# Layer 0 of a four-layer chain: two images' score products interleaved with half of the value sums of two parts back, and stores sent together

## The chip, the cores and the metric

One core of one Trainium2 chip runs the whole chain as one program. The metric is the device time of one execution in microseconds (us). Engines are named as in the profile: PE is TensorE's matmul and PEld its weight load, DVE is VectorE, ACT is ScalarE, POOL is GpSimd, SP is SyncE, which here only issues DMAs.

## The reference

The input is four images of 16 channels, 512 by 512, in float32. Four layers follow each other. Layer 0 is window attention with an MLP; layers 1 to 3 are convolutions (a quantised one with batch statistics, a residual pair of 3x3 convolutions, and a 3x3 convolution with an MLP on 128 hidden channels). Only layer 0 is touched by the change:

```python
def _L0_conv_ref(x, ...):
    x = x + depthwise_3x3(x) + pos_b                 # per channel
    xt = tokens(x); shortcut = xt
    win = windows_of_8x8(aff(xt, alpha1, beta1, color1))   # 64 tokens a window
    q, k, v = heads(win @ qkv_w.T + qkv_b)           # 2 heads of 8 channels
    attn = softmax(einsum('bhnd,bhmd->bhnm', q * 8 ** -0.5, k), axis=-1)
    out = einsum('bhnm,bhmd->bhnd', attn, v) @ proj_w.T + proj_b
    x = shortcut + back(out)
    h1 = gelu(aff(x, alpha2, beta2, color2) @ fc1_w.T + fc1_b)
    return x + (h1 @ fc2_w.T + fc2_b)
...
x = layer0(x); x = layer1(x); x = layer2(x); x = layer3(x)
```

There are 4 x 64 x 64 windows of 64 tokens in layer 0.

## The kernel before, in words

**Steps and parts.** Layer 0 (`window_attention`) works in 64 steps. One step holds 64 columns of 8 rows in each of 8 strips of the four images. The partitions are four groups of 32, called quads: quad u is image u, and it holds two strips of 16 channels. The strips of one image make four pairs `vv`. A step is cut into eight parts k = 0 to 7: part k is strip pair k // 2 and four of its eight windows, for all four images and both strips.

**One part.** `scores(k)` makes 16 score products, one for each image u and window jj. Each reads 32 rows (quad u) and all 128 columns of the array, and writes 128 columns of `bank(u)`; images 0 and 1 share the PSUM tile `pairs[0]`, images 2 and 3 share `pairs[1]`. ACT then takes the exponential of each pair into the tile `e`. `values(k)` turns the values with four 128x128 transposes into a bank, and ACT or DVE copies them into one of three tiles `yts`, beside columns of ones. `attend(e, k)` makes the 32 sums of values and of weights: each reads 64 rows (one strip, w = 0 or 1) and 32 columns (one image) and writes to one of two banks, 4 and 5 for even k, 6 and 7 for odd k. `divide` transposes both banks on DVE (the tile `a`), takes the reciprocal of the sums on DVE, and multiplies on POOL; `turn_back` transposes the quotient on DVE into `o`.

Since the operands are float32, the trace shows each of these products as two passes: a weight load and a matmul, twice. A product of 32 rows and 128 columns is shown as the shape 32*128, one of 64 rows and 32 columns as 64*32.

**The order.** The engines' queues follow the order in which the Python code emits (`manual_schedule`). In the step's loop over k = 1 to 7 the order is:

```python
es[k] = scores(k, n)
values(k)
attend(es[k - 1], k - 1)
ts[k - 1] = divide(k - 1, n, nc.gpsimd)
if 1 < k < 7:
    turn_back(ts[k - 2], k - 2)
if k % 2 and more:
    turn_keys(ys[n + 1], k // 2)
highest_output()
send(5)
```

`turn_keys` issues eight DMAs from SP that write the keys of the next step into `y2` once part k has been read. `send(5)` issues up to five stores of the finished output tile `xo`, from SP. `highest_output` takes one maximum of the output on DVE into `peak`, over 512 values a partition (eight of them for every two steps). Before the loop the step runs `values(0)`, `scores(0)` and `output` (the second matmul of the MLP of the step before, line 432, whose sums DVE writes to `xo`, line 437). After the loop come `attend` of part 7, the remaining divisions, and a stretch of products of 32 rows and 32 columns: depthwise taps (`depthwise`, line 287) and queries (`query`, line 319) for later steps, the projection (`project`, line 409) and the first matmul of the MLP (`hidden`, line 421). ACT changes its table of functions twice in a step, before and after the exponentials.

**Lines of the profile.** Line 353 is the score product, 361 the exponential, 338 the transpose of the values, 344 and 346 their copy on ACT and on DVE, 374 the sums, 389, 394 and 396 the three parts of `divide`, 403 `turn_back`, 452 `highest_output`, 90 a store, 310 a DMA of `turn_keys`. Lines 1047 to 1217 are the matmuls of layers 1 to 3.

Of the kernel before, what the change touches and what calls it, by code (L numbers as in the profile page):

```python
# [12 lines left out]
F32 = mybir.dt.float32  # L13
BF16 = mybir.dt.bfloat16
AF = mybir.ActivationFunctionType
# [9 lines left out]
B, C, H, W = 4, 16, 512, 512  # L25
P = 128
# [5 lines left out]
WS = 8  # L32
# [111 lines left out]
def window_attention(ctx: ExitStack, tc, xw, x1, hots, m, v, peak):  # L144
# [14 lines left out]
    nc = tc.nc  # L159
    U = V = 4  # L160
    BW = 64
# [10 lines left out]
    pairs = [ps.tile([P, 2, 512], F32, name=f"pair{i}") for i in range(2)]  # L172
    singles = [ps.tile([P, 512], F32, name=f"bank{i}") for i in range(4)]

    def bank(i):
        return pairs[i // 2][:, i % 2, :] if i < 4 else singles[i - 4]

    def quad(i):
        return slice(32 * i, 32 * i + 32)
# [81 lines left out]
    px = ctx.enter_context(tc.tile_pool(name="w0x", bufs=2))  # L261
# [6 lines left out]
    y2 = pa.tile([P, V, NJ, 2, T], F32, name="y2")  # L268
    nc.gpsimd.memset(y2, 0.0)
    g = pa.tile([P, V, NJ, NH, T], F32, name="g")  # L270
    o = pa.tile([P, V, NJ, NH, T], F32, name="o")
    most = pa.tile([P, STEPS], F32, name="most")
    yts = [pa.tile([P, 4 * U, 3, C], F32, name=f"yt{i}") for i in range(3)]
# [59 lines left out]
    def values(k):  # L333

        vv, jl = k // 2, 4 * (k % 2)
        b, t = bank(4 + 2 * (k % 2)), yts[k % 3]
        for jj in range(4):
            nc.tensor.transpose(  # L338
                b[:, P * jj : P * jj + P],
                y2[:, vv, jl + jj].rearrange("p w t -> p (w t)"), m("ident"),  # L340
            )
        src = b.rearrange("p (a w c) -> p a w c", w=2, c=C)
        if 0 < k < 7:
            nc.scalar.copy(t[:, :, 0:3:2], src)
        else:
            nc.vector.tensor_copy(t[:, :, 0:3:2], src)  # L346

    def scores(k, n):

        vv, jl = k // 2, 4 * (k % 2)  # L350
        for i, jj in ((0, 0), (0, 1), (1, 0), (0, 2), (1, 1), (0, 3), (1, 2), (1, 3)):
            for u in (2 * i, 2 * i + 1):
                nc.tensor.matmul(  # L353
                    bank(u)[:, P * jj : P * jj + P],
                    y2[quad(u), vv, jl + jj].rearrange("p w t -> p (w t)"),
                    g[quad(u), vv, jl + jj].rearrange("p h t -> p (h t)"),
                    start=True, stop=True,
                )
        e = px.tile([P, U, 4, P], F32, tag="e", name=f"e{n}_{k}", bufs=3)
        for i in range(2):  # L360
            nc.scalar.activation(  # L361
                e[:, 2 * i : 2 * i + 2].rearrange("p u j t -> p u (j t)"),
                pairs[i], AF.Exp,
            )
        return e

    def attend(e, k):

        t = yts[k % 3]
        for jj in range(4):  # L370
            for u in range(U):
                for w in range(2):
                    half = slice(64 * w, 64 * w + 64)
                    nc.tensor.matmul(  # L374
                        bank(4 + 2 * (k % 2) + w)[quad(u), P * jj : P * jj + P],
                        t[half, U * jj + u, w : w + 2].rearrange("p d c -> p (d c)"),
                        e[half, u, jj, :],
                        start=True, stop=True,
                    )

    def part(t, k):
        vv, jl = k // 2, 4 * (k % 2)
        return t[:, vv, jl : jl + 4].rearrange("p j h t -> p (j h t)")

    def divide(k, n, engine):

        a = px.tile([P, 1024 + 2 * C], F32, tag="a", name=f"a{n}_{k}")
        for w in range(2):
            nc.vector.transpose(a[:, 512 * w : 512 * w + 512], bank(4 + 2 * (k % 2) + w))  # L389
        top = a.rearrange("p (w n) -> p w n", w=2)[:, :, 0:512]  # L390
        top = top.rearrange("p w (b c) -> p w b c", c=32)[:, :, :, 0:C]
        low = a[:, C : 1024 - C].rearrange("p (w n) -> p w n", w=2)[:, :, 0 : 512 - C : 32]
        r = px.tile([P, 2, 16], F32, tag="r", name=f"r{n}_{k}")
        nc.vector.reciprocal(r, low)  # L394
        t = px.tile([P, 16, 2, C], F32, tag="t", name=f"t{n}_{k}", bufs=3)
        engine.tensor_tensor(  # L396
            t.rearrange("p b w c -> p w b c"), top,
            r.unsqueeze(3).to_broadcast([P, 2, 16, C]), ALU.mult,
        )
        return t  # L400

    def turn_back(t, k):
        nc.vector.transpose(part(o, k), t.rearrange("p b w c -> p (b w c)"))
# [25 lines left out]
    def output(y, xo, hids, us, banks, n):  # L429

        for k, (vv, hd) in enumerate(hids):
            nc.tensor.matmul(
                bank(banks[k // 4])[quad(vv)], m("fc2"), hd, start=True, stop=True
            )
        at = BW * (n % 2)
        for u, i in zip(us, banks):
            nc.vector.tensor_tensor(  # L437
                xo[:, u, :, at : at + BW].rearrange("p a (j x) -> p a j x", x=WS),
                by_window(bank(i)), by_window(y[:, u]), ALU.add,
            )  # L440
        if n % 2:
            store(xo, n // 2, us)
# [6 lines left out]
    def highest_output(k=1):  # L449
        for _ in range(min(k, len(largest))):  # L450
            xo, i = largest.pop(0)
            nc.vector.tensor_reduce(
                peak[:, i : i + 1], xo, AX.XY, ALU.max, apply_absolute_value=True
            )

    def store(xo, k, us):
        i, cb = divmod(k, NQ)
        for u in us:
            for a in range(2):
                half = slice(WS // 2 * a, WS // 2 * a + WS // 2)  # L460
                largest.append((xo[:, u, half], 2 * (U * k + u) + a))
            for strip in range(2 * V):
                stores.append((xo[C * strip : C * strip + C, u], u, SR * strip + WS * i, cb))

    def send(k, queues=None):
        for _ in range(min(k, len(stores))):
            src, u, r, cb = stores.pop(0)
            _store_block(nc, x1, src, u, r, slice(XW * cb, XW * cb + XW), queues)
# [40 lines left out]
    for n in range(STEPS):  # L509
        more, ahead = n + 1 < STEPS, n + 2 < STEPS  # L510
        taken, asked = [0] * U, [0] * V

        def block(what, i, b, scalar=False):
            at = i % 4
            if what == "q" and more:
                query(ys[n + 1], asked[at], at, b, scalar)
                asked[at] += 1
            elif what == "d" and ahead:
                depthwise(n + 2, taken[at], at)
                taken[at] += 1  # L520
                if taken == [9] * U:
                    ys[n + 2] = position(n + 2)

        values(0)
        es, ts = {0: scores(0, n)}, {}
        if last:

            output(*last)
        for k in range(1, 8):
            es[k] = scores(k, n)  # L530
            values(k)
            attend(es[k - 1], k - 1)
            ts[k - 1] = divide(k - 1, n, nc.gpsimd)
            if 1 < k < 7:
                turn_back(ts[k - 2], k - 2)
            if k % 2 and more:
                turn_keys(ys[n + 1], k // 2)
            highest_output()
            send(5)
        nc.scalar.preload_act_table_set("gelu_and_others")  # L540
        attend(es[7], 7)
        ts[7] = divide(7, n, nc.gpsimd)
        for k in (5, 6, 7):
            turn_back(ts[k], k)
        free = iter((4, 5, 6, 7, 4, 5))
        for i, what in enumerate("qqddddqqqqdddddd"):
            block(what, i, bank(next(free)) if what == "q" else None, True)
        if more:
            highest(n + 1)
        highest_output()  # L550
        y = ys.pop(n)
        project(y)
        if n % 2 == 0:
            xo = px.tile([P, U, WS, XW], F32, tag="xo", name=f"xo{n}", bufs=1)
        if not more:
            flag = bounded()

        hids, units = [], itertools.cycle((6, 7, 4, 5))  # L560
        for i, what in enumerate("ddddhdhddhqhddhqhddhdhddhdhddhdhddhdhddddhdh"):
            if what == "h":
                q = len(hids)
                hids.append(hidden(y, q // 4, i % 4, bank(next(units)), n))
                if not more and q in (5, 9, 13):
                    u = q // 4 - 1
                    output(y, xo, hids[q - 5 : q - 1], (u,), (u,), n)
                    send(8, queues)
            else:
                block(what, i, bank(next(units)) if what == "q" else None)  # L570
        if n + 4 < STEPS:
            xts[n + 4] = load(n + 4)
        if more:
            nc.scalar.preload_act_table_set("natural_log_exp_and_others")
        last = (y, xo, hids, range(U), (5, 4, 6, 7), n)
# [797 lines left out]
```

## Time and profile before

| What | Value |
|---|---|
| median of 3 runs | 5752.89 us (5740.05 to 5767.73) |
| profiled execution | 5755.15 us, its span 5753.4 us |
| mean granted TensorE clock of it | 0.987 of full speed |
| layer 0 in the span | the first 3.27 ms |
| busy: PE, DVE, ACT, POOL | 95%, 65%, 61%, 12% of the span |
| steps of layer 0 | 64, of 49.8 us each |

The profile is of one execution. A line of the timeline gives the start and the length of a group of like instructions, in us, then engine, line, operation, output and inputs, and in square brackets how long the engine was idle before it and what ended that. A line of the windows gives, for a stretch of the span, the busy time of each engine with its number of instructions, the granted TensorE clock (PEclk, 1.00 is full speed), the share of the DMA engines and their rate. Matmuls overlap, so the busy time of PE tells that a matmul was under way, not how much of the array it used.

### The profile page before, as it was taken

The page shows a single profiled execution, that of the slowest core. Times are in us where ns is not written, and L with a number is a line of the kernel's source. Part 1 is how long each engine was busy: PE and PEld are TensorE (multiplying, and loading weights), DVE is VectorE, ACT ScalarE, POOL GpSimd, SP SyncE. Part 2 cuts the span into 40 slices and gives each one's busy share as a digit, 9 for nine tenths or more (in the row PEclk, how much of TensorE's full clock was granted, in tenths as well). Part 3 has the DMA queues.
Part 4 walks back from the last instruction along what each step waited for, and adds up shares of the span by engine and source line. Part 5 has one row for each costly group of instructions (what it writes and reads, how often), then busy time and mean ns, then how long its engine had stood idle before and what let it go on. Part 6 is the DMA issues. An engine that isn't in the chain of part 4 may idle for free. (4 is left out here: it accounts for less than half of the span.)

```text
span 5753.4 us, 268539 instructions
## 1 busy us (share of the span) xinstructions
PE 5477.8 (95%) x120912; PEld 2921.8 (51%) x120912; DVE 3734.7 (65%) x5806; ACT 3491.1 (61%) x4739; POOL 707.3 (12%) x692
## 2 busy tenths in 40 slices
PE   7999999999999999999999776999999999999999
PEld 5666666666666666666666433322222322223222
DVE  4666666666666666666666565676676766767666
ACT  3777767777777777677777554444444444444444
POOL 1111111111111111111111253000000000000000
PEclk9999999999999999999999898999999999999999
DMA  2332323333332323333332497776777777677774
GB/s 79 70 79 67 76 65 78 74 74 76 71 79 68 81 62 76 73 73 76 71 78 48 96 257 202 177 173 175 176 174 177 174 174 176 173 177 174 174 175 110
DMA packets 626194, 677.47 MB, mean 118 GB/s; under 512 B 355856, under 2 KB 485008, under 8 KB 616848
## 3 DMA queue, kind: packets, MB, share of 16 engines
q1 hardware_dynamic: 624240, 658.76, 47.6%
q8 instruction: 953, 15.61, 1.2%
q14 instruction: 201, 1.65, 0.1%
q0 software_dynamic: 512, 1.05, 0.1%
q10 hardware_dynamic: 288, 0.39, 0.0%
HBM read 222.45 MB, written 134.48 MB: 62 GB/s over the span
## 5 line engine op out<-in xcount | busy, mean ns | idle before, releaser
L361 ACT ACTIVATE e<-pair 128x1024 f32<-128x1024 f32 x1024 | 992.8, 1022 | 449.2 <-PE pair L353 448.5
L287 PE MATMUL pair<-x,taps 32*32 32x512 f32 x18432 | 1081.7, 600 | 3.7 <-issue 2.3
L1205 ACT ACTIVATE hid<-tb,vec 128x512 f32<-128x512 f32 x1024 | 646.8, 684 | 630.7 <-PE tb L1197 630.7
L389 DVE STREAM_TRANSPOSE a<-bank 128x512 f32<-128x512 f32 x1024 | 669.8, 692 | 354.2 <-PE bank L374 327.6
L396 POOL TENSOR_TENSOR t<-a,r 128x512 f32<-128x512 f32 x512 | 542.0, 1059 | 2679.3 <-DVE r L394 2615.6
L426 ACT ACTIVATE hid<-bank,f1b 128x512 f32<-128x512 f32 x1024 | 648.1, 687 | 346.0 <-PE bank L421 282.2
L353 PE MATMUL pair<-g,y 32*128 32x128 f32 x16384 | 764.0, 288 | 31.1 <-ACT y L298 25.3
L353 PEld LDWEIGHTS pair<-g,y 32*128 32x128 f32 x16384 | 650.8, 188 | 192.5 <-issue 76.1
L421 PE MATMUL bank<-y,fc_e 32*32 32x512 f32 x8192 | 738.4, 606 | 1.0 <-DVE y L414 1.0
L1207 DVE TENSOR_SCALAR hid<-tb,vec 128x512 f32<-128x512 f32 x1024 | 718.0, 744 | 27.2 <-PE tb L1197 26.9
L374 PE MATMUL bank<-e,yt 64*32 64x128 f32 x32768 | 611.8, 276 | 29.7 <-DVE yt L346 21.1
L1197 PE MATMUL tb<-ye,mat 32*128 32x512 f32 x4096 | 586.2, 640 | 0.0
L287 PEld LDWEIGHTS pair<-x,taps 32*32 32x32 f32 x18432 | 493.4, 103 | 175.5 <-issue 71.2
L374 PEld LDWEIGHTS bank<-e,yt 64*32 64x32 f32 x32768 | 466.9, 106 | 129.0 <-issue 101.9
L1217 PE MATMUL tb<-hid,mat 128*32 128x512 f32 x4096 | 466.0, 595 | 0.0
L1122 PE MATMUL tb<-zo,cw 64*32 64x512 f32 x3096 | 368.2, 601 | 16.7 <-issue 8.9
L338 PE MATMUL bank<-mat,y 128*128 128x128 f32 x2048 | 340.3, 289 | 44.1 <-DVE xo L437 44.1
L1122 PE MATMUL tb<-xo,cw 64*32 64x512 f32 x3096 | 360.3, 592 | 3.7 <-issue 2.2
L1122 PE MATMUL tb<-ho,cw 64*32 64x512 f32 x3072 | 358.0, 593 | 4.6 <-issue 3.0
L1122 PE MATMUL tb<-ze,cw 64*32 64x512 f32 x3072 | 362.2, 601 | 0.0
L1122 PE MATMUL tb<-he,cw 64*32 64x512 f32 x3072 | 357.9, 593 | 0.0
L1122 PE MATMUL tb<-xe,cw 64*32 64x512 f32 x3072 | 355.9, 593 | 0.0
(180 smaller groups left out, 6809.9 us busy)
## 6 DMA issues: line engine op xcount, KB each, us to landing
x<-in_xw_dram SPq DMA_DIRECT2D x64, 1320.0 KB
zo<-ze SPq DMA_DIRECT2D x512, 128.5 KB
ho<-he SPq DMA_DIRECT2D x512, 128.5 KB
xo<-xe SPq DMA_DIRECT2D x512, 128.5 KB
y<-y SPq DMA_DIRECT2D x2048, 32.0 KB
tx<-x SPq DMA_DIRECT2D x256, 256.0 KB
out_dram<-xe SPq DMA_DIRECT2D x128, 512.0 KB
x<-xo SPq DMA_DIRECT2D x1008, 64.0 KB
```

What stands on the lines that cost most here:

```text
L287: nc.tensor.matmul(bank(u)[quad(vv)], taps[quad(u), tap, :], xts[n][quad(u), vv, dy : dy + WS, dx : dx + BW], start=tap == 0, stop=tap == 8,)
L353: nc.tensor.matmul(bank(u)[:, P * jj : P * jj + P], y2[quad(u), vv, jl + jj].rearrange("p w t -> p (w t)"), g[quad(u), vv, jl + jj].rearra ...
L361: nc.scalar.activation(e[:, 2 * i : 2 * i + 2].rearrange("p u j t -> p u (j t)"), pairs[i], AF.Exp,)
L374: nc.tensor.matmul(bank(4 + 2 * (k % 2) + w)[quad(u), P * jj : P * jj + P], t[half, U * jj + u, w : w + 2].rearrange("p d c -> p (d c)"), ...
L389: nc.vector.transpose(a[:, 512 * w : 512 * w + 512], bank(4 + 2 * (k % 2) + w))
L396: engine.tensor_tensor(t.rearrange("p b w c -> p w b c"), top, r.unsqueeze(3).to_broadcast([P, 2, 16, C]), ALU.mult,)
L421: nc.tensor.matmul(b[quad(k)], fc1[quad(vv), quad(k)], y[quad(vv), u, :], start=True, stop=True,)
L426: nc.scalar.activation(hd, b, AF.Gelu, bias=f1b)
L1122: nc.tensor.matmul(p[r][_quad(2 * f + w)], weights[_half(r), odd, dx, :], src[_half(r), f, dx : dx + W], start=dx == 0, stop=dx == 2,)
L1197: nc.tensor.matmul(p[q], w1[_quad(q), 1 - par, :], inner(src)[_quad(q), f, :], start=True, stop=True,)
L1205: nc.scalar.activation(hd, p[q], AF.Relu, bias=v("l3_b1"))
L1207: nc.vector.tensor_scalar(hd, p[q], v("l3_b1"), 0.0, ALU.add, ALU.max)
```

## The change

Part k is now done in two halves i = 0 and 1. Half i makes the scores of images 2i and 2i + 1, and between them the sums of part k - 2 for one strip, w = 1 - i: for each window two score products, then four sums. The scores of half 0 read rows 0 to 63, the sums beside them rows 64 to 127; in half 1 it is the other way round. The exponential of the pair, the DVE transpose of the bank of that strip, and in half 0 the value transposes, the maximum of the output (in every second part) and `turn_back` of part k - 3 follow. The sums lag two parts behind the scores, not one, so that the sums of parts 6 and 7 come after the loop. The value transposes use the other pair of banks, their copy is on ACT for all parts but part 0. The maxima of the output are listed when DVE has the output of a step (four a step, of 64 columns and 8 rows, in place of eight every second step, of 128 columns and 4 rows). The 32 stores of an output tile are issued together at k = 1, ahead of the DMAs of `turn_keys`.

```diff
     def values(k):
 
         vv, jl = k // 2, 4 * (k % 2)
-        b, t = bank(4 + 2 * (k % 2)), yts[k % 3]
+        b, t = bank(4 + 2 * ((k + 1) % 2) if k else 4), yts[k % 3]
...
-        if 0 < k < 7:
+        if k:
             nc.scalar.copy(t[:, :, 0:3:2], src)
...
+    def add_up(e, k, jj, u, w):
+        half = slice(64 * w, 64 * w + 64)
+        nc.tensor.matmul(
+            bank(4 + 2 * (k % 2) + w)[quad(u), P * jj : P * jj + P],
+            yts[k % 3][half, U * jj + u, w : w + 2].rearrange("p d c -> p (d c)"),
+            e[half, u, jj, :],
+            start=True, stop=True,
+        )
...
+        for u in us:
+            largest.append((xo[:, u, :, at : at + BW], 2 * (U * (n // 2) + u) + n % 2))
...
-            for a in range(2):
-                half = slice(WS // 2 * a, WS // 2 * a + WS // 2)
-                largest.append((xo[:, u, half], 2 * (U * k + u) + a))
...
         for k in range(1, 8):
-            es[k] = scores(k, n)
-            values(k)
-            attend(es[k - 1], k - 1)
-            ts[k - 1] = divide(k - 1, n, nc.gpsimd)
-            if 1 < k < 7:
-                turn_back(ts[k - 2], k - 2)
+            e = es[k] = new_e(k, n)
+            a = new_a(k - 2, n) if k > 1 else None
+            for i in range(2):
+                for jj in range(4):
+                    for u in (2 * i, 2 * i + 1):
+                        score(k, u, jj)
+                    if k > 1:
+                        for u in range(U):
+                            add_up(es[k - 2], k - 2, jj, u, 1 - i)
+                probable(e, i)
+                if k > 1:
+                    lanes(a, k - 2, 1 - i)
+                if i == 0:
+                    values(k)
+                    if k % 2 == 0:
+                        highest_output()
+                    if k > 2:
+                        turn_back(ts[k - 3], k - 3)
+            if k > 1:
+                ts[k - 2] = quotient(a, k - 2, n)
+            if k == 1:
+                send(8 * U)
             if k % 2 and more:
                 turn_keys(ys[n + 1], k // 2)
-            highest_output()
-            send(5)
         nc.scalar.preload_act_table_set("gelu_and_others")
-        attend(es[7], 7)
-        ts[7] = divide(7, n, nc.gpsimd)
+        for k in (6, 7):
+            attend(es[k], k)
+            ts[k] = divide(k, n)
```

`score` is one score product as in `scores` before, `probable` the exponential of one pair, `lanes` the DVE transpose of one bank, `quotient` the reciprocal and the product on POOL. The numbers computed stay the same, and so do the counts of matmuls and of the larger DVE, ACT and POOL instructions in two steps, but for one copy that moves from DVE to ACT.

More of the change, by code (lines that the diff above doesn't have):

```diff
@@ L346, in values, with score, probable, new_e @@
             nc.vector.tensor_copy(t[:, :, 0:3:2], src)
+    def score(k, u, jj):
+        vv, j = k // 2, 4 * (k % 2) + jj
+        nc.tensor.matmul(
+            bank(u)[:, P * jj : P * jj + P],
+            y2[quad(u), vv, j].rearrange("p w t -> p (w t)"),
+            g[quad(u), vv, j].rearrange("p h t -> p (h t)"),
+            start=True, stop=True,
+        )
+    def probable(e, i):
+        nc.scalar.activation(
+            e[:, 2 * i : 2 * i + 2].rearrange("p u j t -> p u (j t)"), pairs[i], AF.Exp
+        )
+    def new_e(k, n):
+        return px.tile([P, U, 4, P], F32, tag="e", name=f"e{n}_{k}", bufs=3)
     def scores(k, n):
-        vv, jl = k // 2, 4 * (k % 2)
         for i, jj in ((0, 0), (0, 1), (1, 0), (0, 2), (1, 1), (0, 3), (1, 2), (1, 3)):
             for u in (2 * i, 2 * i + 1):
[L353 to L359, printed above, removed]
+                score(k, u, jj)
+        e = new_e(k, n)
         for i in range(2):
[L361 to L364, printed above, removed]
-        return e
+            probable(e, i)
+        return e
+    def add_up(e, k, jj, u, w):
+        half = slice(64 * w, 64 * w + 64)
+        nc.tensor.matmul(
+            bank(4 + 2 * (k % 2) + w)[quad(u), P * jj : P * jj + P],
+            yts[k % 3][half, U * jj + u, w : w + 2].rearrange("p d c -> p (d c)"),
+            e[half, u, jj, :],
+            start=True, stop=True,
+        )
     def attend(e, k):
-        t = yts[k % 3]
         for jj in range(4):
@@ L372, in attend @@
                 for w in range(2):
[L373 to L379, printed above, removed]
+                    add_up(e, k, jj, u, w)
     def part(t, k):
@@ L383, in part, with new_a, lanes, quotient @@
         return t[:, vv, jl : jl + 4].rearrange("p j h t -> p (j h t)")
[L385 to L389, printed above, removed]
+    def new_a(k, n):
+        return px.tile([P, 1024 + 2 * C], F32, tag="a", name=f"a{n}_{k}")
+    def lanes(a, k, w):
+        nc.vector.transpose(a[:, 512 * w : 512 * w + 512], bank(4 + 2 * (k % 2) + w))
+    def quotient(a, k, n):
         top = a.rearrange("p (w n) -> p w n", w=2)[:, :, 0:512]
@@ L395, in divide @@
         t = px.tile([P, 16, 2, C], F32, tag="t", name=f"t{n}_{k}", bufs=3)
-        engine.tensor_tensor(
+        nc.gpsimd.tensor_tensor(
             t.rearrange("p b w c -> p w b c"), top,
@@ L400, in divide @@
         return t
+    def divide(k, n):
+        a = new_a(k, n)
+        for w in range(2):
+            lanes(a, k, w)
+        return quotient(a, k, n)
     def turn_back(t, k):
@@ L529, in window_attention @@
         for k in range(1, 8):
-            es[k] = scores(k, n)
-            values(k)
-            attend(es[k - 1], k - 1)
-            ts[k - 1] = divide(k - 1, n, nc.gpsimd)
-            if 1 < k < 7:
-                turn_back(ts[k - 2], k - 2)
+            e = es[k] = new_e(k, n)
[3 more added lines that the diff above has]
+                    for u in (2 * i, 2 * i + 1):
+                        score(k, u, jj)
+                    if k > 1:
+                        for u in range(U):
+                            add_up(es[k - 2], k - 2, jj, u, 1 - i)
+                probable(e, i)
+                if k > 1:
[10 more added lines that the diff above has]
+                send(8 * U)
             if k % 2 and more:
                 turn_keys(ys[n + 1], k // 2)
-            highest_output()
-            send(5)
         nc.scalar.preload_act_table_set("gelu_and_others")
-        attend(es[7], 7)
-        ts[7] = divide(7, n, nc.gpsimd)
+        for k in (6, 7):
+            attend(es[k], k)
+            ts[k] = divide(k, n)
         for k in (5, 6, 7):
```

## The prediction

> **What bounds the kernel.** I read the page first: the busy shares, and the row of the granted clock.
>
> ```profile
> PE 5477.8 (95%) x120912; PEld 2921.8 (51%) x120912; DVE 3734.7 (65%) x5806; ACT 3491.1 (61%) x4739; POOL 707.3 (12%) x692
> PEclk9999999999999999999999898999999999999999
> ```
>
> PE always has a matmul under way and nearly the full clock; no other engine passes 65%. So time is won or lost in how densely PE's queue fills the array. Next, the groups of instructions:
>
> ```profile
> L353 PE MATMUL pair<-g,y 32*128 32x128 f32 x16384 | 764.0, 288 | 31.1 <-ACT y L298 25.3
> L374 PE MATMUL bank<-e,yt 64*32 64x128 f32 x32768 | 611.8, 276 | 29.7 <-DVE yt L346 21.1
> ```
>
> PE hardly idles before either: the halves that the change puts side by side stand in a dense stream already. A score pass fills a quarter of the array, a sum pass an eighth. Then the timeline of one part:
>
> ```profile
> 1519.58 1.09 PEld L374 LDWEIGHTS bank<-e,yt 64*32 64x32 f32 x64 [0.17 <-issue]
> 1519.58 1.35 PE L374 MATMUL bank<-e,yt 64*32 64x128 f32 x64
> ...
> 1520.86 1.15 PEld L353 LDWEIGHTS pair<-g,y 32*128 32x128 f32 x32 [0.20 <-issue]
> 1520.86 1.34 PE L353 MATMUL pair<-g,y 32*128 32x128 f32 x32
> ...
> 1522.14 0.66 PE L338 MATMUL bank<-mat,y 128*128 128x128 f32 x4
> 1522.72 0.89 PEld L374 LDWEIGHTS bank<-e,yt 64*32 64x32 f32 x64 [0.17 <-issue]
> ```
>
> At every change of shape even the weight load stands still for 0.17 to 0.20 us, with nothing to wait for. Single starts say why. From the last matmul of one shape to the first of the next it takes 199 ns from sums to scores (384 cases, nearly all 196 to 200), 200 from scores to transposes, 201 from transposes to sums. Within a shape rounds follow every 110 to 112 ns, and weights load ahead. The 199 ns count from the very last sum even where that started 24 to 134 ns after the one before, although it reads rows 64 to 127 and the first score rows 0 to 31. In layer 3, from the score-like shape 32*128 to 64*32, it is 517 or 518 ns after a last matmul on rows 96 to 127, and the next reads rows 0 to 63. So the whole array empties at a change of shape, also where the rows are apart.
>
> **Switches.** Each half becomes four groups of two scores, each followed by four sums: eight changes of shape a half, where a whole part had three. Cost at full clock, from the starts:
> - Two scores: second pass 214 ns after the first, second tile 7 later, then 199: 420 ns.
> - Four sums: second pass 134 ns after the first, fourth tile 18 later, then 199: 351 ns.
> - A part: 8 x 771 ns = 6.17, and 0.59 for the transposes as now: 6.76 us. Before, parts 2 to 7 take 3.10 us each (mean of 62 steps: scores of part 2 start 10.20 us into a step, sums of part 6 end at 28.82).
>
> Nothing hides this: DVE, ACT and POOL finish sooner and wait for PE. The step:
> - Up to part 1, 6.47 us as now. Part 1 has only scores on two tiles: 1.09 + 0.59 + 1.0 = 2.7 us, where it took 3.73 with `attend(0)` and with 0.74 us of waits for line 437.
> - Parts 2 to 7: 6 x 6.76 = 40.6.
> - `attend(6)` and `attend(7)`: 2 x 1.11 = 2.2.
>
> The 32x32 stretch then starts at 52.0 us in place of 30.49: 21.5 us a step, 1,376 us for 64 steps, **7,131 us** on the profiled 5755.15 (2 us over its span, and 0.04% from the median).
>
> **The clock.** The granted clock changes only at multiples of 3.41 us. Windows of that length, pairs of one and its next:
>
> ```profile
> 1514.29:1517.70 3.41, 1.69 (x70) 1.31 (x68) 2.37 (x4) 2.53 (x3) 0.00 (x0) 1.00 0.79 316
> 1517.70:1521.12 3.42, 3.42 (x118) 2.73 (x108) 1.74 (x4) 2.06 (x3) 1.06 (x1) 1.00 0.20 38
> ...
> 2111.62:2115.04 3.42, 1.50 (x68) 1.31 (x68) 2.46 (x4) 0.94 (x2) 0.00 (x0) 1.00 0.86 349
> 2115.04:2118.45 3.41, 3.41 (x54) 2.67 (x36) 1.67 (x3) 0.93 (x2) 1.05 (x1) 0.50 0.19 34
> ...
> 3190.23:3193.65 3.42, 2.84 (x42) 0.64 (x40) 3.15 (x5) 1.06 (x2) 0.00 (x0) 1.00 0.22 40
> 3193.65:3197.06 3.41, 3.41 (x48) 1.04 (x32) 0.75 (x1) 1.75 (x4) 0.00 (x0) 0.50 0.53 94
> ```
>
> The third has PE busy 2.84 us of 3.42 and still loses half the clock; the first, busy 1.69, keeps it. What tells them apart is how much of the array was at work: 42 passes of a sixteenth each at 0.427 us make 1.12 us of whole array, 33%; the second pair's 64 sums and 4 transposes at 0.107 us make 37.5%; the first, with two score passes more, 39%. Over all windows of the 64 steps (90 to 3190 us, passes cut at the edges) the border lies between 36.6% and 37.5% without exception; around the start of the convolutions four windows of 25 to 36% kept the full clock. The changed part has 32 x 1/4 + 64 x 1/8 + 4 = 20 whole passes of 0.107, 2.14 us in 6.76: 32% (28 to 36% by window; before 69%). It falls below the border and should run at half clock.
>
> Of the Trainium skill, "TensorE: Matmul & The Clock Gate", section "Why this matters for your kernels", asks only that there be no idle gaps over some 3 us between bursts. With gaps of 0.2 us the loop would stay at full clock by that, and the sum would be the 7,131 above. The window at 3190 us, with 0.6 us of idle time in all, speaks against it, and the measurement decides.
>
> What half clock costs, from the timeline of a throttled stretch:
>
> ```profile
> 2011.32 1.96 PE L374 MATMUL bank<-e,yt 64*32 64x128 f32 x64
> 2013.21 2.25 PE L353 MATMUL pair<-g,y 32*128 32x128 f32 x32
> 2015.39 0.96 PE L338 MATMUL bank<-mat,y 128*128 128x128 f32 x4
> 2016.27 0.98 PE L374 MATMUL bank<-e,yt 64*32 64x128 f32 x52
> ```
>
> A change of shape takes 347 ns there, a pass 213. Two scores: 373 + 7 + 347 = 727; four sums: 216 + 18 + 347 = 581; a part: 8 x 1.308 + 1.04 = 11.5 us, 1.70 times as much. The gate needs a full low window, so the first 4.5 us of the loop run free: 4.5 + 36.1 x 1.70 = 65.9 us for the loop, 25.3 more. At half clock the loop's share is 18%, so it cannot free itself. The stretch after it reaches 45% even at half clock and frees it after some 4 us: 1.8 more. A step grows by 21.5 + 25.3 + 1.8 = 48.6 us, 64 steps by 3,110: **8,865 us**.
>
> **Other edits.** The copy of part 7's values goes from DVE (0.68 us) to ACT (0.59), under PE. The maxima (0.64 us each) stay four a step on average; three lie beside the loop. The stores in one go put 32 x 0.44 = 14 us on SP ahead of `turn_keys` in every second step. Those 32 DMAs take 0.6 to 1.4 us each, up to some 31 us, and are wanted from the next step on: 45 us of SP in a step of 70 to 100 stays covered; in a step of 48 it would be just covered, and the last keys would then hold up the scores. Storing early ends DVE's wait for `xo` (117 us in 20 cases, of which PE felt 44), already counted in part 1. After the loop DVE has `quotient(5)` and two divisions, about 1.7 us more than now, before the projection, beside 4.1 us of 32x32 products and one more `attend`: between 0 and 0.5 us a step. I take 0 and leave 30 us to the range.
>
> **Rivals.**
> - *No gate.* The array empties, but the gate counts something else than array share. For it: the four exceptions at the start of the convolutions, and that PE is never idle 0.3 us. 7,131 us.
> - *Rows apart run together (faster).* The array empties only for tiles whose rows meet, so scores flow beside sums. A half is then 0.107 + 8 x 0.112 and 0.09 to empty, 1.09 us; a part 2.77, six 16.6 in place of 18.6; part 1 saves 1.0; the later `attend` gives back 0.5: 2.5 us a step, about 5,600. ACT needs 2.53 us a part and DVE 2.72, so half may be lost: I put 5,640. It decides if a pair of groups costs under some 325 ns. Against it: 199 and 517 ns, to the nanosecond, where rows are apart. Starts 5 to 7 ns apart are in the trace only within one shape. By the Trainium skill, "TensorE: Matmul & The Clock Gate", section "Part 3: Packing small matmuls — row/col tiling", tiles with other rows start some 4 ns apart, without a word on shape; that would give this rival's time.
> - *In between.* The gate opens and closes by windows, or a change of shape costs half: 6,000 to 8,000.
>
> That the change doesn't do what it says is excluded: PE's order in the changed program is two scores, four sums, throughout.
>
> **How the numbers follow.** Half clock 0.66, no gate 0.23, in between 0.06, rows apart 0.05. The predicted time is the first, 8,865. Its own bounds: 20 ns on each of 6,144 groups is 120 us, the entry into and exit from the gate 2 us a step is 130: with 30 for the projection, 8,600 to 9,150. The range must reach to "no gate", 7,131 less 100: 7,030 to 9,150. A difference of 0.5% is about what a measurement of this kernel can tell. Faster 0.05, same 0.01, slower 0.94.
>
> **What would show it.** Right: parts 2 to 7 of 6.8 us at full clock or 11.5 at half; starts of sums 420 ns after scores and of scores 351 after sums, or 727 and 581; PEclk near 0.7 in layer 0 (nearly 1 if no gate); ACT and DVE as busy in us as before, at a lower share. Wrong: score and sum starts 5 to 10 ns apart, or parts under 3 us.

## The result

The changed kernel takes 8773.06 us (median of 4 runs, 8759.49 to 8777.31), where the kernel before takes 5760.31 us in the same comparison: 1.523 times as long, with an interval of 1.518 to 1.528. The forecast was 8,865 us in a range of 7,030 to 9,150. The profiled execution has a span of 8770.0 us, 3,017 us more than before, and a mean granted clock of 0.76 (before 0.987).

The busy shares and the granted clock, from the page of the kernel after:

```profile
PE 8574.3 (98%) x120912; PEld 4382.3 (50%) x120912; DVE 3767.2 (43%) x5742; ACT 3603.5 (41%) x4803; POOL 705.9 (8%) x692
PEclk7676667666666666666667666766799999999999
```

PE runs as many instructions as before, and DVE, ACT and POOL are busy for about as many microseconds (ACT for 112 more, of which the 64 copies that it takes over from DVE, 0.59 us each, are some 38); only their shares fall. PE is "busy" for 98% of the span and still has a clock of 6 or 7 tenths through the whole of layer 0. A high busy share and a low clock together are the mark of this change. The groups that it rearranges:

```profile
L350 PE MATMUL pair<-g,y 32*128 32x128 f32 x16384 | 2571.7, 428 | 28.2 <-ACT y L298 25.6
L350 PEld LDWEIGHTS pair<-g,y 32*128 32x128 f32 x16384 | 1667.8, 264 | 1193.1 <-issue 1083.4
L377 PE MATMUL bank<-e,yt 64*32 64x128 f32 x32768 | 2125.0, 401 | 0.0
```

Scores and sums go from 764.0 and 611.8 us of busy time to 2571.7 and 2125.0. The matmuls still show almost no idle time, because the last matmul of a group is listed as under way until after the next group starts (in the timeline below a group of sums is listed with 0.42 us, and the next scores start 0.36 us after it). The stall is seen one row lower: the weight load stands idle for 1193.1 us, nearly all of it "issue", waiting for nothing that the profile shows.

The timeline of PE in part 2 of one step of the kernel after:

```profile
2695.36 0.42 PE L377 MATMUL bank<-e,yt 64*32 64x128 f32 x8
2695.72 0.49 PE L350 MATMUL pair<-g,y 32*128 32x128 f32 x4
2696.14 0.42 PE L377 MATMUL bank<-e,yt 64*32 64x128 f32 x8
2696.49 0.49 PE L350 MATMUL pair<-g,y 32*128 32x128 f32 x4
...
2699.14 0.80 PE L350 MATMUL pair<-g,y 32*128 32x128 f32 x4
2699.86 0.65 PE L377 MATMUL bank<-e,yt 64*32 64x128 f32 x8
2700.44 0.80 PE L350 MATMUL pair<-g,y 32*128 32x128 f32 x4
```

From one group's start to the next: 0.36 us after sums and 0.42 after scores at first, 0.58 and 0.72 from 2699 us on, though the instructions are the same. The windows around that moment (columns: PE, PEld, DVE, ACT and POOL busy, then the granted clock):

```profile
2695.00:2698.00 3.00, 3.00 (x49) 1.76 (x48) 0.78 (x2) 0.88 (x3) 0.00 (x0) 1.00 0.17 33
2698.00:2701.00 3.00, 3.00 (x32) 1.69 (x28) 1.07 (x2) 0.82 (x1) 1.05 (x1) 0.55 0.02 5
2701.00:2704.00 3.00, 3.00 (x28) 1.61 (x24) 0.81 (x2) 1.02 (x1) 0.00 (x0) 0.50 0.00 0
```

PE is busy for all 3.00 us in each window, and the clock falls to half. Half clock lasts to the end of the loop. The exit, from an earlier step:

```profile
2645.00:2657.00 12.00, 12.00 (x108) 6.57 (x110) 2.38 (x4) 2.63 (x3) 1.05 (x1) 0.50 0.03 5
2657.00:2668.00 11.00, 11.00 (x293) 7.40 (x289) 6.95 (x12) 5.41 (x8) 3.17 (x3) 0.67 0.12 23
2668.00:2680.00 12.00, 12.00 (x379) 8.47 (x354) 6.22 (x8) 7.76 (x13) 0.00 (x0) 1.00 0.02 4
```

The loop of that step ends at 2659.4 us, and the two `attend` after it at 2663.4. A mean clock of 0.67 over the middle window is a third of it, some 3.7 us, at full clock, so the clock was released within a microsecond of the end of the attends.

### The profile page after: what moved, and what is told of

Its sections match the earlier page's. It is cut to its first block, busy times and chain, and to the rows that moved or that the text cites. A ratio compares the mean times of both kernels' runs of the same rounds, so it can differ in the third digit from the quotient of the medians.

```text
span 8770.0 us, 268981 instructions
## 1 busy us (share of the span) xinstructions
PE 8574.3 (98%) x120912; PEld 4382.3 (50%) x120912; DVE 3767.2 (43%) x5742; ACT 3603.5 (41%) x4803; POOL 705.9 (8%) x692
## 3 DMA queue, kind: packets, MB, share of 16 engines
q8 instruction: 953, 15.61, 0.8%
## 5 line engine op out<-in xcount | busy, mean ns | idle before, releaser
L350 PE MATMUL pair<-g,y 32*128 32x128 f32 x16384 | 2571.7, 428 | 28.2 <-ACT y L298 25.6
L358 ACT ACTIVATE e<-pair 128x1024 f32<-128x1024 f32 x1024 | 1041.2, 1023 | 3126.0 <-PE pair L350 3116.3
L350 PEld LDWEIGHTS pair<-g,y 32*128 32x128 f32 x16384 | 1667.8, 264 | 1193.1 <-issue 1083.4
L399 DVE STREAM_TRANSPOSE a<-bank 128x512 f32<-128x512 f32 x1024 | 716.1, 709 | 3424.8 <-PE bank L377 3415.1
L377 PE MATMUL bank<-e,yt 64*32 64x128 f32 x32768 | 2125.0, 401 | 0.0
L377 PEld LDWEIGHTS bank<-e,yt 64*32 64x32 f32 x32768 | 792.4, 136 | 660.2 <-issue 607.8
L338 PE MATMUL bank<-mat,y 128*128 128x128 f32 x2048 | 486.3, 380 | 0.0
L338 PEld LDWEIGHTS bank<-mat,y 128*128 128x128 f32 x2048 | 311.1, 189 | 199.1 <-issue 137.4
L319 PE MATMUL bank<-y,wg 32*32 32x512 f32 x4032 | 364.4, 629 | 0.1
```

The lines of the kernel that those rows point to most:

```text
L338: nc.tensor.transpose(b[:, P * jj : P * jj + P], y2[:, vv, jl + jj].rearrange("p w t -> p (w t)"), m("ident"),)
L350: nc.tensor.matmul(bank(u)[:, P * jj : P * jj + P], y2[quad(u), vv, j].rearrange("p w t -> p (w t)"), g[quad(u), vv, j].rearrange("p h t - ...
L358: nc.scalar.activation(e[:, 2 * i : 2 * i + 2].rearrange("p u j t -> p u (j t)"), pairs[i], AF.Exp)
L377: nc.tensor.matmul(bank(4 + 2 * (k % 2) + w)[quad(u), P * jj : P * jj + P], yts[k % 3][half, U * jj + u, w : w + 2].rearrange("p d c -> p ...
```

## The experiments

Each kernel is measured beside the kernel before on the same chip, and ratios are to that. Times of parts and steps are means over 62 steps, from the starts of single matmuls in each trace; a step counts from its first transpose. The share of the array is worked out as in the prediction: for each pass its rows times its columns, as a part of 128 x 128, for the time in which its columns stream (0.107 us for 128 of them at full clock).

**Do the rows matter?** The sums beside the scores take the strip on the same rows as the scores, where the change puts them on the others.

```diff
-                            add_up(es[k - 2], k - 2, jj, u, 1 - i)
+                            add_up(es[k - 2], k - 2, jj, u, i)
...
-                    lanes(a, k - 2, 1 - i)
+                    lanes(a, k - 2, i)
```

> The changed kernel with the strips swapped: the sums beside the scores of a half now read the same 64 rows as those scores, not the other 64. If the whole array empties at every change of shape, rows do not matter: 420 and 353 ns a group at full clock, 725 and 582 at half, and the time of the changed kernel, 8,773 us within 0.5%. If rows that are apart still save something, the groups get longer; 20 ns on each of 6,144 groups would be 120 us (1.4%) or more at half clock.

8772.50 us, ratio 1.529 (1.523 to 1.535): the kernel after, whose interval it overlaps. The two groups, from its page:

```profile
L350 PE MATMUL pair<-g,y 32*128 32x128 f32 x16384 | 2574.6, 428 | 28.6 <-ACT y L298 25.7
L377 PE MATMUL bank<-e,yt 64*32 64x128 f32 x32768 | 2126.8, 401 | 0.0
```

428 and 401 ns, as in the kernel after. Keeping the rows apart buys nothing while the shapes differ.

**What does the clock gate count?** Every sum is done twice, which adds work and no change of shape.

```diff
                         for u in range(U):
-                            add_up(es[k - 2], k - 2, jj, u, 1 - i)
+                            for w in (0, 1):
+                                add_up(es[k - 2], k - 2, jj, u, w)
```

> The changed kernel with more work and no more changes of shape: in each half the sums of both strips are made, so every sum is made twice (the second time with the same result). A group of eight sums on eight tiles takes 372 ns at full clock where four took 353. If the gate counts the share of the array at work, a part has 2.14 + 0.86 = 3.0 us of whole array in 8 x 0.79 + 0.59 = 6.9 us, 43%, and without the transposes 40%, above the border of 36%: the clock stays full in layer 0 and the time falls to about 7,190 us, though there is more to do. If the gate counts idle time or changes of shape, the clock stays at half and the time is 8,800 to 8,950.

7236.24 us, ratio 1.261 (1.256 to 1.267), clock 0.986. The page and the timeline of this kernel:

```profile
PE 7031.0 (97%) x145488; PEld 3631.3 (50%) x145488; DVE 3754.6 (52%) x5742; ACT 3572.7 (49%) x4803; POOL 707.5 (10%) x692
PEclk7999999999999999999999999999999999999999
```

```profile
1515.02 0.49 PE L350 MATMUL pair<-g,y 32*128 32x128 f32 x4
1515.44 0.45 PE L377 MATMUL bank<-e,yt 64*32 64x128 f32 x16
1515.82 0.49 PE L350 MATMUL pair<-g,y 32*128 32x128 f32 x4
1516.24 0.45 PE L377 MATMUL bank<-e,yt 64*32 64x128 f32 x16
```

With 24,576 more matmul instructions the program is 1,537 us faster than the kernel after. Each group start still costs the change of shape (420 ns after scores, 380 after eight sums), but the clock stays full to the end of the loop. A part holds 28 whole-array passes of 0.107 us in 6.99 us, 43% of the array, where the change holds 20 in 6.76, 32%. So it is not whether PE is busy that decides. A count of passes does not fit either. The convolutions of the kernel before, from 3,400 us to the end, keep the clock:

```profile
3400.00:5753.00 2353.00, 2271.03 (x31512) 713.59 (x31503) 1606.36 (x2343) 1134.77 (x1616) 87.97 (x90) 0.99 0.70 175
```

That is 46 passes in 3.41 us, fewer than the 50 with which the change loses it; and in the kernel of one shape, further down, windows of 127 to 130 passes with 25% of the array in use lose it too, where this kernel keeps it with 80 passes of the same length. Of the measures tried here the share of the array is the one that fits. The Trainium skill, "TensorE: Matmul & The Clock Gate", section "Why this matters for your kernels", asks for no idle gaps over some 3 us. In the steps of layer 0 of the kernel after PE is never idle for 1 us, and it is throttled all the same, so here that rule is not enough.

This run also gives a price for the rival without a gate: 7,236 less 6 x 64 x 0.23 us for the added sums is 7,148 us, against the 7,131 worked out.

**At the border.** Groups of two windows: four scores, then eight sums. Half as many changes of shape, with a share of 35% in the halves without value transposes and 42% in those with.

```diff
-                for jj in range(4):
-                    for u in (2 * i, 2 * i + 1):
-                        score(k, u, jj)
+                for j0 in range(0, 4, 2):
+                    for jj in range(j0, j0 + 2):
+                        for u in (2 * i, 2 * i + 1):
+                            score(k, u, jj)
                     if k > 1:
-                        for u in range(U):
-                            add_up(es[k - 2], k - 2, jj, u, 1 - i)
+                        for jj in range(j0, j0 + 2):
+                            for u in range(U):
+                                add_up(es[k - 2], k - 2, jj, u, 1 - i)
```

> The changed kernel with groups twice as long: the scores of two windows (four), then their sums (eight), so half the changes of shape. At full clock four scores take 644 ns and eight sums 571, a part 4 x 1.215 + 0.59 = 5.45 us. Share of the array: 39% over a part, but 35% in a window that holds no transposes, just under the border (35.5 to 36.6%). Gate by share: half clock again, about 9.7 us a part and 8,050 us. No gate for it: 6,630. If the loss were simply in proportion to the changes of shape: half of it, 7,270.

7736.29 us, ratio 1.349 (1.341 to 1.358), clock 0.819: between the expectations with and without a gate. The timeline of one step:

```profile
1546.55 0.64 PE L377 MATMUL bank<-e,yt 64*32 64x128 f32 x16
1547.12 0.71 PE L350 MATMUL pair<-g,y 32*128 32x128 f32 x8
1547.77 0.64 PE L377 MATMUL bank<-e,yt 64*32 64x128 f32 x16
1548.34 0.71 PE L350 MATMUL pair<-g,y 32*128 32x128 f32 x8
...
1552.04 1.08 PE L377 MATMUL bank<-e,yt 64*32 64x128 f32 x16
1553.04 1.22 PE L350 MATMUL pair<-g,y 32*128 32x128 f32 x8
```

A pair of groups takes 643 + 571 ns at full clock (a part 5.44 us) and 1,152 + 1,008 at half (9.69 us). The loop starts at full clock in each step and falls at different points: the part from the transposes of part 2 to those of part 3 takes 5.67 us on average, the next two 7.65 and 9.17, the last ones 9.69. Windows of 3.41 us with 34.8 to 37.1% of the array in use were followed by either clock. So the step down to half is real, but its border is a band, not a line.

**Four windows to a group**, the same edit with `range(0, 4, 4)`: eight scores, then sixteen sums.

> The changed kernel with no interleaving inside a half: its eight scores, then its sixteen sums. At full clock 1.09 and 1.12 us, a part 2 x 2.21 + 0.59 = 5.0 us. Share of the array 39% even without the transposes, above the border: full clock in layer 0 and about 6,450 us. In proportion to the changes of shape: a quarter of the loss, 6,510. If scores and sums on rows apart ran side by side once each is a long run: a part of under 3 us and less than 5,760.

6379.31 us, ratio 1.113 (1.107 to 1.118), clock 0.987. Its timeline:

```profile
1520.65 1.08 PE L377 MATMUL bank<-e,yt 64*32 64x128 f32 x32
1521.66 0.66 PE L338 MATMUL bank<-mat,y 128*128 128x128 f32 x4
1522.25 1.16 PE L350 MATMUL pair<-g,y 32*128 32x128 f32 x16
```

Scores 1.09 us, sums 1.01, a part 4.78 (45% of the array): the clock stays.

The three sizes together price a change of shape. At full clock a part of the change takes 6.76 us with 17 changes of shape, groups of two 5.44 with 9, groups of four 4.78 with 5: 0.165 us for each change, whether taken from the first and second or from the second and third. The groups say what it is made of. Two, four and eight scores take 420, 643 and 1,090 ns to the next group, and four, eight and sixteen sums 352, 571 and 1,008: 109 to 112 ns a round, and beside that a fixed 197 ns for a group of scores and 133 for one of sums, 165 on average. By that price, groups of four without their two extra changes would take 4.45 us, against 3.10 before with 3. The other 1.35 us belong to the halves: a half's scores stand on two of the four row groups and its sums on one strip of two, so that eight rounds of 112 ns carry half as many products. Of the 3.66 us by which a part grows at full clock, 14 changes are thus 2.31 and half-empty rounds 1.35. The 3.10 us of before also hold some 0.3 us of waits (its rounds and changes alone make 2.8), so the rounds may cost 1.65 and the waits that are gone give 0.3 back. This split is worked out, not run by itself.

**Is it the change of shape?** The score product is cut into four of 32 columns, and the sums read 32 rows, so that both have the shape 32*32; the order is that of the change.

```diff
-        nc.tensor.matmul(
-            bank(u)[:, P * jj : P * jj + P],
-            y2[quad(u), vv, j].rearrange("p w t -> p (w t)"),
...
+        for c in range(4):
+            nc.tensor.matmul(
+                bank(u)[quad(c), P * jj : P * jj + P],
+                y2[quad(u), vv, j].rearrange("p w t -> p (w t)")[:, quad(c)],
...
-        half = slice(64 * w, 64 * w + 64)
+        half = slice(64 * w, 64 * w + 32)
```

> The changed kernel with scores and sums in one shape of the array, 32 rows by 32 columns: a score product is cut into four of 32 columns, and a sum reads 32 of its 64 rows, so half of the keys are left out of the sums. The order, two scores and then four sums, and the rows apart stay. If the change of shape is what empties the array, scores and sums now start a few ns apart inside a half: 8 rounds of 110 ns and one change, 1.1 us a half, a part 2.8 to 3.0 us (ACT needs 2.53, DVE 2.72), full clock, 5,650 to 5,810 us. If alternating scores and sums, or their banks, costs the time whatever the shape, 7,000 us or more.

7067.01 us, ratio 1.226 (1.223 to 1.230), clock 0.83: far from the 5,650 to 5,810 that I expected. The timeline and the instruction queue tell two things apart:

```profile
1988.77 0.33 PE L351 MATMUL pair<-g,y 32*32 32x128 f32 x4
1990.63 0.31 PE L351 MATMUL pair<-g,y 32*32 32x128 f32 x4 [1.53 <-issue]
1990.66 0.31 PE L378 MATMUL bank<-e,yt 32*32 32x128 f32 x4
1990.69 0.36 PE L351 MATMUL pair<-g,y 32*32 32x128 f32 x8
```

```profile
q8 instruction: 1336, 21.89, 1.4%
```

The mechanism holds. Sums follow scores by 30 ns at 1990.66 and scores follow sums by 30; the median from the last start of one to the first of the other is 11 to 12 ns, at both clocks, where the kernel after has 200 and 347. From sums to transposes, where the shape still changes, it is 198 and 347. So it is the change of shape that empties the array. The Trainium skill, "TensorEngine Tiling (Array Packing)", section "Key Properties", says that a change of tiling mode drains TensorE; these runs agree, and show 200 ns from the last start to the next.

The time does not follow, because of something else: PE now stops for 0.4 to 2.4 us at a time for "issue", with nothing in these views to wait for. The kernel has 170,064 matmul instructions in place of 120,912, and its instruction queue carries 21.89 MB in place of 15.61. No part from 2 on takes under 4.3 us; the median of those at full clock is 5.14 where 2.8 to 3.0 were expected, which leaves 33% of the array in use, and half clock comes on top.

The packets of the instruction queue in the same trace tie this to the supply of instructions. Of the 304 pauses over 0.1 us before scores and sums, 98% end 1.2 to 1.6 us after such a packet has landed, as against 9 to 12% of moments or matmul starts taken at random. The packets hold 16 KB and land hardly ever less than 3.4 us apart (1% of the intervals are under 3.38 us, in this trace and in that of before). The added matmuls and their weight loads come to 64 bytes each; a part has 392 of them, 1.53 packets, and at 3.4 us a packet that is 5.2 us, an estimate that meets the 5.14. No run varies the supply alone, so this is an inference from one trace, though a close one.

In this kernel windows with 26 to 34% of the array in use were followed by either clock, so the border is not at the same share for every mix of products.

**The other edits alone**, in the order of the kernel before: stores together at k = 1, four maxima a step, the copy of part 7 on ACT.

```diff
-        if 0 < k < 7:
+        if k:
...
+            if k % 2 == 0:
+                highest_output()
+            if k == 1:
+                send(8 * U)
             if k % 2 and more:
                 turn_keys(ys[n + 1], k // 2)
-            highest_output()
-            send(5)
```

> The kernel before with the other edits alone: 32 stores together at k = 1, four maxima of the output in every step, the copy of part 7's values on ACT. The order of scores, transposes and sums is that of before. If the prediction's account holds, the waits of DVE for the output tile (117 us, of which PE felt 44) go, and nothing else: about 5,710 us, 0.8% faster. Rival: 14 us of stores on SP ahead of the key DMAs, in a step of 49 us, make the last keys late: scores of parts 6 and 7 wait, and the time is the same or up to 2% more.

5694.27 us, ratio 0.993 (0.991 to 0.994): 0.7% faster. Then the stores alone, with the maxima and the copy as before:

```diff
+            if k == 1:
+                send(8 * U)
             if k % 2 and more:
                 turn_keys(ys[n + 1], k // 2)
             highest_output()
-            send(5)
```

> The kernel before with one edit, the 32 stores of an output tile together at k = 1; the maxima stay eight in every second step. If the wait of DVE for the output tile is what the side edits took away, this alone does it: 0.7% faster, 5,695 to 5,710 us. If spreading the maxima over both steps did it, nothing to 0.2%.

5717.32 us, ratio 0.991 (0.989 to 0.993), as much as all the side edits by these intervals. What DVE's additions into `xo` waited for, in the kernel before and then with the stores together (us in total, times, longest):

```profile
DVE xo L437 <- PE bank L432: 137.7, 108, 5.3
DVE xo L437 <- DMA x<-xo: 117.0, 20, 7.9
```

```profile
DVE xo L437 <- PE bank L432: 190.3, 185, 3.4
```

The wait for the stores, 117.0 us in 20 cases, is gone from the list (the wait for PE's sums grows by 53), and PE's part of it with it: the transposes of part 1 start 7.68 us into a step in place of 8.42, and a step takes 49.06 us in place of 49.78, 46 us in 64 steps.

**The lag without the interleaving.** All of the change but the side-by-side order: whole parts, sums two parts back.

```diff
...
+            es[k] = scores(k, n)
+            values(k)
+            if k % 2 == 0:
+                highest_output()
             if k > 1:
-                ts[k - 2] = quotient(a, k - 2, n)
+                attend(es[k - 2], k - 2)
+                ts[k - 2] = divide(k - 2, n)
+            if k > 2:
+                turn_back(ts[k - 3], k - 3)
```

> The changed kernel without the interleaving: whole parts in the order scores, transposes, sums of part k - 2, with the lag of two parts and the other edits of the change. If the loss is all in the changes of shape, it is gone: three of them a part as before, full clock, 5,640 to 5,760 us. It is 5,740 if the lag gains nothing and the second attend after the loop costs 0.5 us a step on top of the side edits; 5,640 if the lag takes away the waits in a part, which takes 3.10 us before where rounds and changes of shape alone make 2.8. If the lag or the later sums are part of the loss, it is over 5,800.

5809.85 us, ratio 1.012 (1.010 to 1.014), and 116 us over the side edits alone, 1.8 us a step. The end of the loop in its timeline:

```profile
1559.64 1.16 PE L377 MATMUL bank<-e,yt 64*32 64x128 f32 x64
1561.59 1.36 PE L377 MATMUL bank<-e,yt 64*32 64x128 f32 x79 [0.79 <-ACT yt L344]
1563.39 0.95 PE L377 MATMUL bank<-e,yt 64*32 64x128 f32 x49 [0.45 <-issue]
```

Three `attend` now follow the last transposes, 5.00 us in place of 3.59, and part 1, which has lost one, gets no shorter, since the scores of part 2 then wait for the exponentials of part 1 (30.7 us in 63 cases; the wait of 0.79 us for the copy, shown above, is there without the lag too). Together that is 1.36 us; the 32x32 stretch takes 19.37 us in place of 18.91, the other 0.46. The lag is a loss by itself when PE is dense.

**The best version found**: the side edits in the old order, with the four maxima moved into the 32x32 stretch.

```diff
-            if k % 2 == 0:
-                highest_output()
...
-        highest_output()
...
+            if i == 22:
+                highest_output(4)
```

> The kernel before with all side edits, and the four maxima of a step moved from between the parts into the 32x32 stretch, to where DVE idles 5.7 us a step before the position bias. In the side-edits kernel parts with a maximum take 3.21 us and parts without 2.90 to 3.03. If DVE sets the longer ones, three of them shrink by 0.2 to 0.3 us a step: 38 to 58 us less, about 5,645 us, 1.6% faster than before. If ACT sets them (the copy of the values behind two exponentials), the time is that of the side edits, 5,694.

5685.33 us, ratio 0.986 (0.984 to 0.988): 1.4% faster than the kernel before and the lowest ratio of all that ran. The stores alone ran beside it and took 5717.32, 32 us more; the steps of the two traces, 48.61 and 49.06 us, say 29. The maxima find an idle place there, as DVE's longest wait shows, in the kernel before and then in this one:

```profile
DVE y L302 <- PE pair L287: 370.1, 64, 10.5
```

```profile
DVE y L302 <- PE pair L287: 224.5, 64, 10.7
```

The parts of the loop, though, alternate between 3.21 and 2.92 to 3.08 us as with the maxima in the loop (3.21 and 2.90 to 3.03). So DVE's maxima do not set the long parts; what does stays open. The 38 to 58 us expected from moving them did not come: the side edits and this kernel were not measured beside each other, and the steps of their traces, 48.70 and 48.61 us, differ by some 6 us in 64.

## Why the prediction was right

**Switches: right.** From scores to sums 420 ns were predicted and 420 measured at full clock, 727 and 725 at half; from sums to scores 351 and 352 to 353, 581 and 582. The reading that carried it was the fixed 199 to 201 ns at each change of shape in the trace of before, also where the rows were apart. The same rows give the same time, and one shape gives 12 ns: both halves of the claim are shown by a run. What the prediction left unsaid is that its sum under "Switches" holds two costs, the changes and the half-empty rounds; since it was taken from single starts, both were in it.

**The clock: right in its direction and its size.** From the transposes of part 3 to those of part 7 each part takes 11.50 us, as worked out, and 4,213 us of the span are at half clock. Doubling the sums lifts the array's share to 43%, and the clock returns. Of the 47.1 us that a step grew, then, some 24 are the clock (8,773 less 7,236 in 64 steps, without a correction for the doubled sums) and the rest changes of shape and half-empty rounds, less what the stores give back. Where the prediction was too neat is the border: "between 36.6% and 37.5% without exception" held for the trace of before, but with groups of two, windows from 34.8 to 37.1% were followed by either clock, and with one shape from 26 to 34%. (The 33, 37.5 and 39% that it gives for its three pairs count whole passes; cut at the edges, as for its border, they are 24, 36.5 and 37.5.) For the change, at 18% once at half clock, this made no difference. For groups of two it made the whole one.

**The exit from half clock: the term that was off.** The prediction added 1.8 us a step to the 32x32 stretch. Measured, the stretch takes 19.25 us (before 19.30; with the sums doubled, at full clock, 19.31). The prediction let the stretch free the clock, some 4 us in. The two attends before it do that already: their sums stand together and fill the array, and the window that ends half clock, with 36 to 51% of the array in use, lies mostly in them. The clock returns between 1.1 us before and 1.5 us after their end, 0.1 after on average. They take 3.5 us in place of the 2.2 predicted; the loop runs free for 4.8 us where 4.5 were assumed, and ends 1.0 us sooner. Loop and attends together end 77.58 us into a step, where the terms add up to 77.3. So a step is 96.8 us long and not 98.4: 1.6 us in 64 steps, about 100 us, are the whole distance between forecast and result (92 us).

**Stores: right.** PE's 44 us of waits for line 437 were to go, and the stores alone bring 50 us by the ratio of their medians, 46 by the steps. In the change itself this is the start of part 1's transposes, 7.56 us into a step in place of 8.42.

**Later sums and divisions: the right bound, for a mixed reason.** I put 0 to 0.5 us a step on the projection and took 0; the stretch is indeed no longer than before. But with the side edits in the old order it takes 18.91, so the lag costs 0.3 to 0.5 there, and the edits to the maxima and the copy hide it. What the prediction did not ask is what the lag costs at the end of the loop when PE is not slowed down, 1.36 us. In the change this cannot be seen on its own.

**The rivals.** "No gate" has its measured stand-in at 7,148 us and fails by the clock row. "Rows apart run together" fails by the same rows giving the same time; the condition named for it, a pair of groups under some 325 ns, is missed by a pair of 772 ns. "In between" is what groups of two windows do, at 7,736 us, but not the change.

## What to carry to other kernels

Count the changes of matmul shape in PE's order before putting two kinds of small products side by side: each cost 0.165 us here at full clock, also where the rows were apart, and a busy share near 100% does not show it, while an idle weight load with "issue" does. Then work out what share of the whole array the new order keeps at work in windows of 3.4 us: below some 35% the clock was halved in most of these kernels (in the one of one shape below 26 to 34%), and a part of the change then took 1.7 times as long. Small products gain from standing together in long runs of one shape that fill all rows; stores that hold up a buffer are best sent as soon as their data are there.

## What the runs showed of the hardware that was not expected

- More work can be faster: with every sum done twice the program took 7,236 us in place of 8,773, because the array's share rose from 32 to 43% and the clock stayed full.
- A longer instruction stream had a price of its own: with 170,064 matmul instructions PE paused up to 2.4 us at a time, 278 us in all at the two lines of scores and sums, and 98% of the pauses ended 1.2 to 1.6 us after a packet of the instruction queue had landed. The kernel after has no such idle time at its sums (0.0) and none but 28.2 us, nearly all for ACT, at its scores.
- Near the border the granted clock is not settled by the share of one window alone: with groups of two, windows of 34.8 to 37.1% went either way, and with one shape windows of 26 to 34%.
